# One product of the gate placed three sums later in every group, the mask counted earlier, one set of weight sums and two copies placed later

## The chip, the core and the metric

The kernel runs on one core of one Trainium2 chip. Five engines work side by side: TensorE (PE; its weight loads are listed as PEld), VectorE (DVE), ScalarE (ACT), GpSimd (POOL) and SyncE (SP, which only issues transfers here). The metric is the device time of one execution in microseconds, taken as the median of three runs.

## The reference

For 2 x 1024 tokens of 512 features, a layer norm is followed by two branches: a linear layer whose weight is multiplied by a 32 x 32 block mask, and a gated feed-forward layer with 1792 inner features. Their product is added to the input.

```python
xn = _layernorm(x, axis=-1)
# masked linear: a 32x32 block of the weight is kept where its mask sums to more than 0
block_mask = mask.reshape(nb, BLOCK_H, kb, BLOCK_W).astype(jnp.float32).sum(axis=(1, 3)) > 0
...
s = jnp.einsum('bsk,nk->bsn', xn, weight * elem_mask)
# feed-forward
var = jnp.mean(jnp.square(xn), axis=-1, keepdims=True)
nx = xn * jax.lax.rsqrt(var + RMS_EPS) * ln_w
g = jnp.einsum('bsh,ih->bsi', nx, gate_w)
u = jnp.einsum('bsh,ih->bsi', nx, up_w)
f = jnp.einsum('bsi,hi->bsh', jax.nn.silu(g) * u, down_w)
return x + s * silu(f)
```

## The kernel before

**The arithmetic.** All matrices are float32. A matrix product is cut into 2 x 2 blocks and done with seven block products instead of eight, and each of these is again cut into 2 x 2 and done with seven. The outer seven are called q (lists `OUTER` and `BLOCKS`), the inner seven m. One inner product is a 128 x 128 weight times a 128 x 512 operand (128 features by 512 tokens). The price of the saving is sums and differences: of the weights (`inner_a` on POOL, 128 columns at a time, and `outer_a`), of the activations (`outer_b`, `inner_b` on DVE and POOL), and of the products (`instance`, on DVE and ACT).

**The stages.** There are seven groups g of 256 inner features, gate and up together, and an eighth group, the masked linear layer. First the outer products q = 1 and 2 of all eight groups run, then q = 6, 5, 7, 3, 4 of group 0, of group 1 and so on. Each (g, q) is an *instance* j with seven products, so a group in the second stage takes 5 instances or 35 products. Then the down projection follows, seven sets of 25 products (`down_instance`, line 640).

**The order.** It is written out by hand. `at(pos, fn)` files a piece of work under a position; all pieces are sorted by position, and each engine runs its own pieces in exactly that order. One unit of position is one product on PE; instance j has positions 7j to 7j+6 and on, and its products stand at 7j + 0, 2, 3, 4, 6, 8, 12. Position 0 is about 14 us after the start. An instruction that waits holds back everything behind it on its engine, and SP's transfers are such a queue too. In this text "p148" means position 148.

**One instance** (`instance`). Product m = 1 goes to a PSUM bank x; ACT copies it to a bank z (`seed`, L399); m = 5 goes to a bank y, m = 2 is added to z. A copy of a bank is taken before the bank is added to again: m = 6 is added to x, and one position later `snap` (DVE, or ACT where there is nothing to add) writes bank plus an earlier partial result to SBUF; then m = 7 and m = 4 are added to the same bank. The same is done with y. `total` writes the four results. So a later product of the instance must wait until a `snap` or `total` has read its bank. PSUM has three banks of the kind X, two Y, one Z and two V. V serves everything else.

**The gate of a group** (`group`). When the four tiles of one output (R, Hh) are there, `silu` (ACT) puts silu of a gate tile into a V bank, and `h_out` (L463, DVE) multiplies it with the up tile and stores the product to DRAM by a transfer of SP. Output (1, 1) needs another sum first: for q = 7, `summed` adds acc to v5 for its tiles 0 and 1 on DVE and for 2 and 3 on POOL. The dictionary `hpos` holds the position of each `h_out`. `h_sum` (POOL) takes differences of these products, at positions worked out from `hpos`.

**Held copies.** `outer_b_held` lets ACT copy one operand into a V bank (`hold`, L249) and then DVE subtract with it (`outer_b`), 0.9 positions later.

**The mask.** `load_mask` loads four 128 x 512 tiles into the slots q.0 to q.3, free until the first group's blocks are loaded at p83. `mask_rows` (L349, DVE) sums 32 columns at a time; `mask_blocks` (p79.5) does the rest on PE and DVE.

**The start.** Tokens are loaded, normalised on ACT and DVE (L153/L155), transposed on PE (L162), and the first two instances (j = 0, 1) are run with positions of their own (`EARLY`). `inner_b(q, m)` makes the operands of q = 1 and 2: the list at line 777 has them with their positions and engines. `inner_a(0, 1, K, 1)` makes the four weight sums s1, s2, s4, s3 of q = K + 1 on POOL.

Of the kernel before, what the change touches and what calls it, by code (L numbers as in the profile page):

```python
# [31 lines left out]
def tile_masked_linear_gated_ffn(  # L32
# [36 lines left out]
    def at(pos, fn, *args):  # L69
        events.append((pos, len(events), fn, args))  # L70
# [18 lines left out]
    def slots(i, n):  # L89
        return mem[:, i : i + n, :]  # L90
# [3 lines left out]
    def bank(tag, name):  # L94
        return ps.tile([P, W], F32, tag=tag, name=name, bufs=PSB[tag])

    def add(eng, o, a, b, op=ALU.add):
        eng.tensor_tensor(o, a, b, op)  # L98

    dve, pool, act = nc.vector, nc.gpsimd, nc.scalar  # L100
# [150 lines left out]
    def outer_b_held(pos, lag, q, k, n):  # L251
        v = {7: lambda: u12[k, n], 6: lambda: raw[k, n], 5: lambda: raw[2 + k, 2 + n]}[q]
        at(pos - lag, hold, (q, k, n), v)
        at(pos, outer_b, q, k, n, dve)
# [39 lines left out]
    def w_slots(g):  # L294

        return (F["s"], F["s"] + 5) if g % 2 else (F["q"], F["a1"] + 4)
# [59 lines left out]
    def mask_a(v, R, K):  # L356
        v = v.rearrange("p (b j) -> p b j", j=BLK)
        k = keep[:, 2 * R + K, :].unsqueeze(2).to_broadcast([P, 16, BLK])
        nc.gpsimd.tensor_tensor(v, v, k, ALU.mult)

    def inner_a(g, part, k0=0, n=2):

        if part == 1:
            i, si, qs = F["a1"] + 2 * (g % 3), F["s"] + 2 * (g % 2), (1, 2)
        else:
            i, si, qs = *w_slots(g), BLOCKS
        a, s = slots(i + k0, n), slots(si + k0, n)
        a11, a21, a12, a22 = (a[:, :, k * P : (k + 1) * P] for k in range(4))
        s1, s2, s3, s4 = (s[:, :, k * P : (k + 1) * P] for k in range(4))
        for k in range(n):  # L370
            aop[g, qs[k0 + k]] = {1: a11[:, k], 2: a12[:, k], 3: s4[:, k], 4: a22[:, k],
                                  5: s1[:, k], 6: s2[:, k], 7: s3[:, k]}
        return [lambda: add(pool, s1, a21, a22), lambda: add(pool, s2, s1, a11, ALU.subtract),
                lambda: add(pool, s4, a12, s2, ALU.subtract), lambda: add(pool, s3, a11, a21, ALU.subtract)]
# [72 lines left out]
    def group(g, where):  # L447
        def tiles(i):
            return lambda k: mem[:, i + k, :]

        acc, v5, c1 = tiles(F["acc"] + 4 * (g % 2)), tiles(F["v5"] + 4 * (g % 2)), tiles(F["c1"] if g % 2 else F["vc"])
        vc = tiles(F["tmp"] + 2 if g % 2 else F["vc"])
        h11 = tiles(F["a1"])
        gate = {}

        def silu(key, t):
            gate[key] = bank("V", f"gate_{g}_{key[2]}")
            nc.scalar.activation(gate[key], t(), AF.Silu)  # L458

        hs, hpos = {}, {}  # L460

        def h_out(key, a, b, n):
            nc.vector.tensor_mul(a(), gate[key], b())  # L463
            hs[key] = a()
            q = {(0, 0): 1, (1, 0): 2, (1, 1): 3}.get(key[:2])
            if q:
                nc.sync.dma_start(h_dram[HD[q], g, n], a())

        def done(R, Hh, tiles):

            ready = {}

            def after(i, pos):
                r, n = divmod(i, 2)
                if g == G:
                    at(pos + 1, lambda: nc.sync.dma_start(s_dram[2 * R + r, 2 * Hh + n], tiles(i)))
                    return
                ready[i] = pos
                if n in ready and n + 2 in ready:
                    key = (R, Hh, n)  # L480
                    p = max(ready[n] + 1.2, ready[n + 2] - 0.5, SILU)
                    at(p, silu, key, lambda: tiles(n))
                    hpos[key] = max(p, ready[n + 2]) + 1.3
                    at(hpos[key], h_out, key, lambda: tiles(n), lambda: tiles(n + 2), n)
            return after

        def summed(dst, src, into, then=None, engines=(pool,) * 4):

            def after(i, pos):
                at(pos + 1.2, lambda: add(engines[i], into(i), dst(i), src(i)))  # L490
                if then:
                    then(i, pos + 3.2)
            return after

        nothing = lambda i, pos: None
        setup = {
            1: (None, acc, nothing),
            2: (acc, c1, done(0, 0, c1)),
            6: (acc, acc, nothing),
            5: (None, v5, summed(v5, acc, vc)),  # L500
            7: (acc, acc, summed(v5, acc, v5, done(1, 1, v5), (dve, dve, pool, pool) if g < G else (pool,) * 4)),
            3: (vc, vc, done(0, 1, vc)),
            4: (acc, acc, done(1, 0, acc)),
        }
        for q in setup:
            instance(where[g, q], g, q, *setup[q])

        def h_sum(q, n, tile_of, a, b):

            o = hs[q, n] = tile_of()  # L510
            add(pool, o, hs[a + (n,)], hs[b + (n,)], ALU.subtract)
            nc.sync.dma_start(h_dram[HD[q], g, n], o)

        sums, rest = slots(F["acc"] + 4 * (g % 2), 4), 7 * where[g, BLOCKS[0]]
        at(7 * where[g, 1] + 15, lambda: nc.sync.dma_start(acc_dram[g], sums))
        at(rest - (14 if g else 6), lambda: nc.sync.dma_start(sums, acc_dram[g]))
        if g < G:
            def again():
                nc.sync.dma_start(slots(F["a1"], 2), h_dram[HD[1], g].rearrange("n p w -> p n w"))
                hs.update({(0, 0, n): h11(n) for n in range(2)})  # L520
            at(rest + 24, again)
            pos = 0
            for n in (1, 0):
                for q, t, i, a, b in ((5, vc, n + 2, (0, 1), (0, 0)), (7, v5, n + 2, (1, 1), (0, 1)),
                                      (6, vc, n, (1, 1), (5,))):
                    pos = max(pos, hpos[0, 1, n], hpos[1, 1, n]) + 1.45
                    at(pos, h_sum, q, n, lambda t=t, i=i: t(i), a, b)
            for n in (1, 0):
                pos = max(pos, hpos[1, 0, n]) + 1.45
                at(pos, h_sum, 4, n, lambda n=n: acc(n + 2), (1, 0), (6,))  # L530
# [195 lines left out]
    T = lambda us: (us - 14.0) / 0.86  # L726
# [19 lines left out]
    def plan(pos, step, todo):  # L746
        for i, fn in enumerate(todo):
            at(pos + step * i, fn)
# [26 lines left out]
        at(T((9.75, 10.3, 10.85, 12.05)[c]), evacuate, 0, c, act)  # L775
        at((5.6, T(15.6), 6.0, 3.14)[c], evacuate, 1, c, act)
    for pos, q, m, eng in ((1.1, 1, 5, dve), (1.87, 1, 6, dve), (2.56, 1, 7, dve), (3.95, 2, 5, dve), (2.7, 1, 4, pool),
                           (4.6, 2, 6, dve), (7.2, 2, 7, dve), (5.0, 2, 4, pool)):
        at(pos, inner_b, q, m, eng)
    for q in (1, 2):  # L780
        for k in (0, 1):
# [20 lines left out]
        at(61 + k, outer_b, 4, k, 1, pool)  # L802
        at(67 + 1.3 * k, outer_b, 4, k, 0, pool)
    for pos, lag, q, k, n in ((51.0, 0.9, 5, 0, 1), (53.0, 0.9, 5, 1, 1), (57.2, 0.9, 7, 0, 0), (58.5, 0.9, 6, 0, 0), (60.3, 0.9, 7, 1, 0),
                              (61.4, 0.9, 6, 1, 0), (64.2, 0.9, 5, 0, 0), (65.6, 0.9, 5, 1, 0)):
        outer_b_held(pos, lag, q, k, n)
    for k in (0, 1):
        for n in (0, 1):
# [12 lines left out]
    for g in range(G + 1):  # L821
        p, rest = 7 * where[g, 1], 7 * where[g, BLOCKS[0]]
        for K in range(2):
            if g > 2:
                at(p - 22, load_a, g, K)
            if g == G:
                at(p - (10.4, 7.3)[K], lambda K=K: mask_a(aq[G, 0, K], 0, K))
            elif g > 1:
                at(p - (10.4, 7.3)[K], scale_a, g, K)
        if g:  # L830
            plan(p - 7, 1, inner_a(g, 1))
        else:
            plan(T(9.9), 0, inner_a(0, 1, 0, 1))
            plan(T(11.9), 0, inner_a(0, 1, 1, 1))
        at(rest - 29, load_block, g)

        def block_sums(g=g):
            for k, fn in enumerate(outer_a(g)):
                todo[g, k] = fn
        at(rest - 20, block_sums)  # L840
        if g == G:
            for k, (R, K) in ((1, (1, 0)), (4, (1, 1)), (0, (0, 0)), (3, (0, 1))):
                at(rest - 20.5, lambda k=k, R=R, K=K: mask_a(wblk[G][k], R, K))
        for k, off in enumerate((-19.9, -19.3, -18.1, -17, -15.95, -15.94, -15.93, -15.3, -13.95)):
            at(rest + off, lambda g=g, k=k: todo[g, k]())
        plan(rest - 13, 2.5, inner_a(g, 2, 0, 5))
# [1 line left out]
        for off, fn in zip((8, 24.6, 26.05, 26.06, 26.07, 27.5, 30), outer_d(f)):  # L848
            at(7 * where[f, BLOCKS[0]] + off, fn)
    for i, (R, K) in enumerate(QUADS):  # L850
        at(50, load_mask, R, K)
        at(62 + 3.5 * i, mask_rows, R, K)
    at(79.5, mask_blocks)
    at(120, rms_store)
    for t in range(NTT):
# [129 lines left out]
```

## Time and profile before

| | |
|---|---|
| median of three runs | 510.44 us (510.37 to 510.63) |
| the profiled execution | 510.38 us |
| its span, first to last instruction | 508.6 us, so 1.8 us lie outside it |
| TensorE clock granted | 0.999 |
| product x, two matmul records (L392) | 595 ns each; alone a pair is listed with 1.02 us, and pairs follow each other every 0.86 us |
| DVE sum with a PSUM input, 128 x 512 (L98) | 683 ns; back to back one starts every 0.60 us |
| DVE product h_out (L463) | 682 ns, 56 of them |
| mask_rows (L349) | 0.67 to 0.68 us, four of them |
| POOL sum 128 x 512 | 1.27 to 1.29 us |
| POOL sum 128 x 128 (first weight sums) | 0.45 to 0.51 us |
| ACT copy to or from a bank | 0.55 to 0.60 us |

PE's records overlap: a float32 product is two records that each begin before the one ahead has ended. So the starts of the products have to be read, not their busy time. In an answer of the timeline a line with x2 is one product, x4 two products; the columns are the start, the time from there to the last end, engine, line, operation, tiles, number of instructions and, in brackets, the idle time ahead of it and what ended it.

### The profile page before, as it was taken

What the parts mean: (1) busy time and instruction counts of PE and PEld (TensorE: products, weight loads), DVE (VectorE), ACT (ScalarE), POOL (GpSimd) and SP (SyncE); (2) the same over time, 40 slices, a digit from 0 to 9 for tenths busy, and PEclk for the clock granted to TensorE, in tenths of its full rate; (3) what the DMA queues carried; (4) which work ended last, traced back from release to release, by engine and by line L of the source; (5) the groups of instructions that cost most, each with busy time, mean ns of one, the idle gap of its engine ahead of it and who ended that gap; (6) DMA issues with size and microseconds to landing.
All of it is one profiled execution on the core that took longest, in us unless ns stands there. A gap on an engine that the chain in (4) does not pass through costs nothing. (4 is left out here: it accounts for less than half of the span.)

```text
span 508.6 us, 4930 instructions
## 1 busy us (share of the span) xinstructions
PE 502.6 (99%) x1237; PEld 227.2 (45%) x1237; DVE 376.4 (74%) x583; ACT 188.4 (37%) x361; POOL 358.6 (71%) x300
## 2 busy tenths in 40 slices
PE   8999999999999999999999999999999999999996
PEld 7444434444444444444444444444444444444444
DVE  6978798776978969697796969969747644377636
ACT  5656776634535363352635334330100101001111
POOL 4628997473786959879596889976672764649960
PEclk9999999999999999999999999999999999999999
DMA  6758866269178495866939566599996798467362
GB/s 206 249 189 337 315 227 253 89 256 321 48 242 310 179 309 198 284 250 225 348 145 312 198 236 231 202 337 378 356 343 244 230 394 307 134 247 254 120 226 84
DMA packets 62221, 124.75 MB, mean 245 GB/s; under 512 B 5968, under 2 KB 13552, under 8 KB 60144
## 3 DMA queue, kind: packets, MB, share of 16 engines
q1 hardware_dynamic: 62048, 124.43, 68.6%
q8 instruction: 10, 0.16, 0.1%
q14 instruction: 19, 0.16, 0.1%
q10 hardware_dynamic: 144, 0.00, 0.0%
HBM read 78.25 MB, written 46.15 MB: 245 GB/s over the span
## 5 line engine op out<-in xcount | busy, mean ns | idle before, releaser
L98 POOL TENSOR_TENSOR mem<-mem 128x512 f32<-128x512 f32 (+4 forms) x261 | 322.3, 1258 | 115.1 <-ACT mem L420 32.3
L392 PE MATMUL x<-mem 128*128 128x512 f32 x448 | 213.8, 595 | 0.7 <-DVE mem L98 0.4
L392 PEld LDWEIGHTS x<-mem 128*128 128x128 f32 x448 | 83.8, 190 | 110.3 <-issue 85.8
L98 DVE TENSOR_TENSOR mem<-x,mem 128x512 f32<-128x512 f32 x137 | 92.5, 683 | 42.6 <-PE x L392 39.1
L392 PE MATMUL y<-mem 128*128 128x512 f32 x224 | 114.7, 593 | 0.1
L640 PE MATMUL dx<-mem 128*128 128x512 f32 x174 | 78.3, 592 | 0.0
L98 DVE TENSOR_TENSOR mem<-mem 128x1536 f32<-128x1536 f32 (+3 forms) x50 | 66.3, 1332 | 6.9 <-PE dx L640 4.4
L98 DVE TENSOR_TENSOR mem<-y,mem 128x512 f32<-128x512 f32 x96 | 65.6, 684 | 6.8 <-PE y L392 5.3
L392 PEld LDWEIGHTS y<-mem 128*128 128x128 f32 x224 | 42.2, 190 | 53.7 <-issue 48.3
L399 ACT COPY z<-x 128x512 f32<-128x512 f32 x54 | 30.9, 572 | 91.9 <-PE x L392 88.9
L392 PE MATMUL z<-mem 128*128 128x512 f32 x112 | 57.4, 594 | 0.0
L640 PEld LDWEIGHTS dx<-mem 128*128 128x128 f32 x174 | 33.1, 190 | 41.6 <-issue 40.7
L640 PE MATMUL dy<-mem 128*128 128x512 f32 x98 | 44.5, 592 | 0.0
L463 DVE TENSOR_TENSOR mem<-gate,mem 128x512 f32<-128x512 f32 x56 | 38.1, 682 | 5.9 <-POOL mem L98 3.6
L458 ACT ACTIVATE gate<-mem 128x512 f32<-128x512 f32 x56 | 33.1, 601 | 24.8 <-DVE mem L98 20.3
L613 POOL TENSOR_TENSOR mem<-mem 128x512 f32<-128x512 f32 x16 | 25.6, 1609 | 14.0 <-DMA mem<-s_dram 13.8
L623 ACT ACTIVATE silu<-mem 128x512 f32<-128x512 f32 x15 | 9.0, 602 | 64.6 <-DVE mem L98 48.3
L392 PEld LDWEIGHTS z<-mem 128*128 128x128 f32 x112 | 21.0, 190 | 26.3 <-issue 23.3
L98 DVE TENSOR_TENSOR mem<-z,mem 128x512 f32<-128x512 f32 x41 | 28.0, 683 | 2.8 <-PE z L392 2.7
L640 PEld LDWEIGHTS dy<-mem 128*128 128x128 f32 x98 | 18.6, 190 | 23.4 <-issue 23.2
L98 DVE TENSOR_TENSOR mem<-dx,mem 128x512 f32<-128x512 f32 x16 | 11.1, 691 | 20.5 <-PE dx L640 20.4
L640 PE MATMUL dz<-mem 128*128 128x512 f32 x56 | 25.2, 592 | 0.0
(85 smaller groups left out, 290.3 us busy)
## 6 DMA issues: line engine op xcount, KB each, us to landing
h_dram<-mem SPq DMA_DIRECT2D x98, 256.0 KB, 2.1
mem<-h_dram SPq DMA_DIRECT2D x28, 768.0 KB, 6.3
mem<-in_gu SPq DMA_DIRECT2D x42, 256.0 KB, 3.9
acc_dram<-mem SPq DMA_DIRECT2D x8, 1024.0 KB, 4.3
mem<-acc_dram SPq DMA_DIRECT2D x8, 1024.0 KB, 5.8
mem<-in_x_t SPq DMA_DIRECT2D x24, 256.0 KB, 5.9
mem<-in_x SPq DMA_DIRECT2D x16, 256.0 KB, 4.4
s_dram<-mem SPq DMA_DIRECT2D x16, 256.0 KB, 5.1
```

The source lines that it names most:

```text
L98: eng.tensor_tensor(o, a, b, op)
L392: nc.tensor.matmul(st[key], weights(g, q, m), operand(q, m), start=first and not (key == "z" and seeded), stop=True, skip_group_check=True)
L399: nc.scalar.copy(st["z"], st["x"])
L458: nc.scalar.activation(gate[key], t(), AF.Silu)
L463: nc.vector.tensor_mul(a(), gate[key], b())
L613: at_later.append(lambda: nc.gpsimd.tensor_tensor(s_tile, s_tile, rms_bc[t], ALU.mult))
L623: nc.scalar.activation(b[0][:, part], y[:, part] if source is None else source(), AF.Silu)
L640: nc.tensor.matmul(st[key], w(), b(), start=first and key != "z", stop=True, skip_group_check=True)
```

## The change

Five edits of positions; no instruction is added, removed or given to another engine.

```diff
-                    hpos[key] = max(p, ready[n + 2]) + 1.3
+                    hpos[key] = max(p, ready[n + 2]) + (3.9 if key == (1, 1, 0) else 1.3)
                     at(hpos[key], h_out, key, lambda: tiles(n), lambda: tiles(n + 2), n)
...
-                           (4.6, 2, 6, dve), (7.2, 2, 7, dve), (5.0, 2, 4, pool)):
+                           (4.6, 2, 6, dve), (9.05, 2, 7, dve), (5.0, 2, 4, pool)):
         at(pos, inner_b, q, m, eng)
...
-                              (61.4, 0.9, 6, 1, 0), (64.2, 0.9, 5, 0, 0), (65.6, 0.9, 5, 1, 0)):
+                              (61.4, 0.9, 6, 1, 0), (65.1, 1.0, 5, 0, 0), (66.3, 1.3, 5, 1, 0)):
         outer_b_held(pos, lag, q, k, n)
...
-            plan(T(11.9), 0, inner_a(0, 1, 1, 1))
+            plan(2.75, 0, inner_a(0, 1, 1, 1))
...
     for i, (R, K) in enumerate(QUADS):
-        at(50, load_mask, R, K)
-        at(62 + 3.5 * i, mask_rows, R, K)
+        at(15 + 1.2 * i, load_mask, R, K)
+        at((46.1, 48.1, 50.2, 52.6)[i], mask_rows, R, K)
```

In every group the `h_out` of output (1, 1), token tile 0, is filed 2.6 positions later, with the transfer it issues; in group 0 that is p146.1 instead of p143.5. The difference `inner_b(2, 7)` goes from p7.2 to p9.05 on DVE. The two held copies of q = 5 move from p63.3 and p64.7 to p64.1 and p65.0 on ACT, the sums that use them from p64.2 and p65.6 to p65.1 and p66.3 on DVE. POOL's weight sums of q = 2, group 0, go from p-2.4 to p2.75. The four mask loads go from p50 to p15.0 to p18.6 on SP, the four counts from p62, 65.5, 69, 72.5 to p46.1, 48.1, 50.2, 52.6 on DVE.

## The prediction

> **What bounds the kernel now.** I read the busy times first, then PE's waits, then the starts on PE's timeline, and at each irregular start the timelines of DVE and ACT.
>
> ```profile
> PE 502.6 (99%) x1237; PEld 227.2 (45%) x1237; DVE 376.4 (74%) x583; ACT 188.4 (37%) x361; POOL 358.6 (71%) x300
> ```
>
> PE is busy 99% of the span, and the list of PE's waits has only 1.3 us at the start and this:
>
> ```profile
> PE x L392 <- DVE mem L98: 0.4, 1, 0.4
> ```
>
> That would leave 0.4 us to win. But the records overlap, so a late product need not leave idle time. In a smooth stretch a product starts every 0.86 us: one has a length of 1.02, two together 1.88. I looked for longer ones. The first kind returns in every group; PE around group 0's gate:
>
> ```profile
> 139.29 1.02 PE L392 MATMUL y<-mem 128*128 128x512 f32 x2
> 140.15 2.12 PE L392 MATMUL x<-mem 128*128 128x512 f32 x4
> 142.11 1.02 PE L392 MATMUL y<-mem 128*128 128x512 f32 x2
> ```
>
> 140.15 to 142.11 is 1.96 for two products that take 1.72: 0.24 lost. The second of the two is p148, which adds to the bank that the `snap` at p145 reads. DVE there:
>
> ```profile
> 137.91 0.68 DVE L463 TENSOR_TENSOR mem<-gate,mem 128x512 f32<-128x512 f32 x1
> 139.21 0.69 DVE L463 TENSOR_TENSOR mem<-gate,mem 128x512 f32<-128x512 f32 x1 [0.61 <-POOL mem L98]
> 139.81 0.68 DVE L98 TENSOR_TENSOR mem<-z,mem 128x512 f32<-128x512 f32 x1
> 140.41 1.28 DVE L98 TENSOR_TENSOR mem<-x,mem 128x512 f32<-128x512 f32 x2
> ```
>
> The `h_out` of (1, 1, 0) stands idle 0.61 us for POOL's sum of tile 2, and the `snap` (first of the pair at 140.41) ends at 141.10, with p148 starting at 141.15. The same 2.12 (2.11 once) stands at 170.43, 200.72, 231.00 and on; the last group is worse:
>
> ```profile
> 322.07 2.29 PE L392 MATMUL x<-mem 128*128 128x512 f32 x4
> 324.20 1.02 PE L392 MATMUL y<-mem 128*128 128x512 f32 x2
> ```
>
> 324.20 - 322.07 = 2.13 against 1.72: 0.41. The second kind is around p66 to p71:
>
> ```profile
> 68.89 1.02 PE L392 MATMUL y<-mem 128*128 128x512 f32 x2
> 69.87 1.12 PE L392 MATMUL z<-mem 128*128 128x512 f32 x2
> 70.83 1.88 PE L392 MATMUL x<-mem 128*128 128x512 f32 x4
> 72.68 1.12 PE L392 MATMUL y<-mem 128*128 128x512 f32 x2
> 73.64 1.96 PE L392 MATMUL x<-mem 128*128 128x512 f32 x4
> 75.44 1.02 PE L392 MATMUL y<-mem 128*128 128x512 f32 x2
> ```
>
> 68.89 to 75.44 is 6.55 for seven products (7 x 0.858 = 6.01): 0.54 lost. At 69.87 PE waits for ACT's `seed` (69.27 to 69.82), which stood behind a `hold` at 68.75; at 72.68 for this `snap`, the last line:
>
> ```profile
> 70.76 0.67 DVE L349 TENSOR_REDUCE mask_sums<-mem 128x16 f32<-128x512 int32 x1
> 71.35 0.68 DVE L98 TENSOR_TENSOR mem<-held,mem 128x512 f32<-128x512 f32 x1
> 71.95 0.68 DVE L98 TENSOR_TENSOR mem<-y,mem 128x512 f32<-128x512 f32 x1
> ```
>
> A mask count and a held sum stand ahead of it. The third is the start: PE's p12 starts at 23.10 after p11 at 21.64 (0.60 lost), waiting for DVE's `total` of p9, which had `inner_b(2, 7)` ahead of it:
>
> ```profile
> 21.67 0.68 DVE L98 TENSOR_TENSOR mem<-mem,pt 128x512 f32<-128x512 f32 x1
> 22.27 0.68 DVE L98 TENSOR_TENSOR mem<-x,mem 128x512 f32<-128x512 f32 x1
> 23.05 0.69 DVE L98 TENSOR_TENSOR mem<-y,mem 128x512 f32<-128x512 f32 x1
> ```
>
> From 324 to 501 PE has no irregular start, so time won before then should arrive at the end.
>
> **What the Trainium skill says.** Perfetto Trace Analysis, Identifying the Most-Contended Engine: PE's busy share is no good measure of headroom, because of pipelining. The trace agrees: 99% hides the losses above. PSUM — Partial Sum Buffer, Engine vs sequencer instructions: the queues of ScalarE, VectorE and GpSimd are strict FIFO; the 0.61 us wait above passing on to a `snap` whose own inputs were ready is just that. The same page, PSUM bank collisions: engines must be kept apart on one bank, reads too; here PE's p148 starts 0.05 after the bank's reader ends. SBUF — State Buffer, Who interferes with whom: DVE's tensor_scalar can contend with GpSimd, a DVE sum with one SBUF input does not. The trace agrees: DVE's halves of `normalise` took 0.44 to 0.61 beside POOL's sums at 14 to 16 us; sums with a PSUM input take 0.68 with POOL busy or idle.
>
> **The change part by part.** PE times are those of before, so each part is a shift.
>
> *The gate's product.* At p146.1 it follows `total` p144, `snap` p145, `total` p146. With DVE starting one sum each 0.60 us and PE's ends known, `total` p144 starts at 138.52, the `snap` at 139.12 (ends 139.80), `total` p146 at 139.72, the product at 140.35; POOL's tile was there at 139.18, so the wait is gone. p148 may start at 141.01, 1.2 after the `snap`. Next on DVE, `total` p147 starts at 140.95 instead of 141.61, so nothing behind is later. The gate's V bank is held until 141.03; its next user, the `silu` at p148.5, started at 142.32. The store moves 1.1 us and past one `h_sum` store on SP (issued 141.93), so to about 142.3; its DRAM tile is read only in the down stage, and `h_sum` positions do not move (p147.65 is already later than p146.1). In group 6 the same sequence gives the `snap` an end of 321.9 against p148's counterpart due at 322.93. Gain 6 x 0.24 + 0.41 = 1.85; bounds 0.87 of it (a small remainder in each group) and all.
>
> *Counts and held copies, where they leave.* The `seed` goes ahead of the `hold`: it starts about 68.75, ends 69.30, due 69.75. On DVE without the count: held sum 69.88 (after a `hold` at 69.27 to 69.86), `snap` p66 at 70.48, ends 71.16, due 72.32; the `snap` of p68 ends 73.56, due 74.0. Gain 0.54, bounds 0.3 and 0.54.
>
> *The counts, where they arrive.* DVE idles 1.08 us before 54.50: the first count fits at 53.32. From there, one start each 0.60: count 55.10, `total` 55.70, `h_out` 56.30, count 56.88, held sum 57.48, `total` 58.08, `snap` 58.86 (its input is the `total`, as now), count 59.46, held sum 60.05, `total` 60.65, `snap` p54 61.25 to 61.93. PE's p57 adds to that bank at 62.02 and needs 0.05 after the reader: some 0.04 of cover. If it is missed, a stall as in the groups, 0.1 to 0.25. I take 0. DVE has caught up by 63.08, where it idled 0.38. The loads: SP has nothing to do between the token loads (17.55) and 24.84, so one mask load leaves at about 18.0 and three after the 1 MB store at 24.84; with some 0.45 us per issue, the weight load at 25.27 leaves 1.4 later. It is used by ACT at about 41, landing was 29.9. Nothing.
>
> *The start.* `inner_b(2, 7)` behind `total` p9 puts that at 21.67, end 22.35, and p12 starts when PE reaches it, 22.50. The next late one is `snap` p10 (bank Y), now third: 22.87 to 23.55 against 23.05 to 23.74. p13 is due 23.36 and gets about 23.62, plus 0.10 in its second half as at every such restart. p14 then comes at 24.58 instead of 24.89: gain 0.31. POOL's sums now run after `inner_b(1, 4)` ends at 18.73, four of 0.5 one after the other, to 20.7; PE needs the first at 20.7 (there at 19.2) and the second at 21.6 (19.7). Without them at 14 to 16, DVE's `normalise` ends up to 0.4 earlier, but the next DVE sum that matters waits for ACT's copy at 16.05 to 16.64: 0.05 more. Together 0.35, bounds 0.15 and 0.6.
>
> Sum: 1.85 + 0.54 + 0.35 = 2.74. Against the profiled 510.38 that is 507.64, with a span of 505.9; the median was 0.06 higher, so **507.7 us**.
>
> **The rivals.** *The gains come only in part:* the counts meet p57, or the start moves its whole wait to `snap` p10. For it: the 0.04 of cover, and a DVE full from 16 to 24 us. Against: each is one stall. 507.7 + 0.25 + 0.3 + some 0.1 = 508.3. *The wait in the groups is replaced:* another reader (ACT's `seed`, or POOL's weights) ends as late as the `snap` did. For it: POOL runs without a gap from 134 to 143. Against: its weights for p149 and p150 were finished at 140.7, and ACT was idle 2 us before the `seed` at 141.21. Only 0.9 remains: 509.5. *Slower:* SP's queue. A mask load that has to wait for a transfer ahead of it (the last token load shows such a wait, ending at 17.53) holds the loads behind it: the weights and the transposed tokens. POOL uses the latter from 40.68 on, and they land from 33.7 on, with 5.8 us at POOL's next weight sums before PE needs those. It decides from a delay of 7 + 5.8 = 13 us on; 17 us would cost 4 on PE, less the 2.7 won, +1.3: 511.7. Nothing in the trace waits so long.
>
> **How the numbers follow.** Forecast 0.74, partial 0.12, replaced 0.08, slower 0.06. Low: everything at its upper bound, 510.44 - 3.0, with a little for the run: 507.2. High: the partial case and 0.5 over it, 508.8; 0.14 is left outside. A change of under 0.2% (1.0 us) would be none that a measurement can tell: 509.5 is 0.18% faster, so of the replaced case 0.06 counts as same and 0.02 as faster; slower 0.06, faster 0.88.
>
> **What would show it.** Right: the 2.12 gone at each group's p148 and groups 30.03 apart rather than 30.28; no brackets of 0.61 at L463; seven even products from 68 to 75; p12 after p11 by 0.86 and a small late start at p13. Wrong: a late p57, about 0.35 less than 62.02; a new long pair in each group; POOL or DVE waiting for transfers from 40 us on.

## The result, and the profile after

The changed kernel takes 507.86 us (median of five runs, 507.54 to 507.97) against 510.63 us for the kernel before, measured beside it (five runs, 510.37 to 511.12). The ratio is 0.9944, with a 95% interval of 0.9930 to 0.9959: faster by 0.4 to 0.7%. The forecast was 507.7 us with a range of 507.2 to 508.8. The profiled span fell from 508.6 to 505.8 us (forecast 505.9).

The busy times of the page, after:

```profile
PE 500.3 (99%) x1237; PEld 228.0 (45%) x1237; DVE 377.2 (75%) x583; ACT 187.6 (37%) x361; POOL 358.9 (71%) x300
```

PE's share is 99% again, though 2.8 us of the span have gone: the share tells nothing here. The starts do. (0.14 of the 2.8 us lie ahead of all moved work: DVE's reciprocal before `normalise`, L143, starts at 13.46 instead of 13.60.) PE's timeline after the change, around group 0's gate:

```profile
138.32 1.02 PE L392 MATMUL y<-mem 128*128 128x512 f32 x2
139.18 1.88 PE L392 MATMUL x<-mem 128*128 128x512 f32 x4
140.90 1.02 PE L392 MATMUL y<-mem 128*128 128x512 f32 x2
```

The pair that was 2.12 long is 1.88, and 139.18 to 140.90 is 1.72, two products without a loss. DVE's timeline there:

```profile
136.95 0.68 DVE L463 TENSOR_TENSOR mem<-gate,mem 128x512 f32<-128x512 f32 x1
137.55 0.68 DVE L98 TENSOR_TENSOR mem<-z,mem 128x512 f32<-128x512 f32 x1
138.15 1.28 DVE L98 TENSOR_TENSOR mem<-x,mem 128x512 f32<-128x512 f32 x2
139.35 0.68 DVE L463 TENSOR_TENSOR mem<-gate,mem 128x512 f32<-128x512 f32 x1
```

No idle time stands in brackets any more: sums start every 0.60 us, and the product (139.35) follows behind three of them. The `snap` that PE waits for is the first of the pair at 138.15. On the page the line of these 56 products shows the wait gone in sum too (it had 5.9 us of idle time, most of it ended by POOL):

```profile
L463 DVE TENSOR_TENSOR mem<-gate,mem 128x512 f32<-128x512 f32 x56 | 38.1, 682 | 1.9 <-ACT gate L458 1.4
```

PE where the counts and held copies were, p65 to p72:

```profile
68.47 1.02 PE L392 MATMUL y<-mem 128*128 128x512 f32 x2
69.32 1.02 PE L392 MATMUL z<-mem 128*128 128x512 f32 x2
70.18 1.88 PE L392 MATMUL x<-mem 128*128 128x512 f32 x4
71.90 1.02 PE L392 MATMUL y<-mem 128*128 128x512 f32 x2
72.76 1.88 PE L392 MATMUL x<-mem 128*128 128x512 f32 x4
74.47 1.02 PE L392 MATMUL y<-mem 128*128 128x512 f32 x2
```

68.47 to 74.47 is 6.00 for seven products: nothing is lost. Three late places remain. PE at the start, p9 to p14:

```profile
20.47 1.10 PE L392 MATMUL y<-mem 128*128 128x512 f32 x2
21.40 1.89 PE L392 MATMUL x<-mem 128*128 128x512 f32 x4
23.45 1.10 PE L392 MATMUL y<-mem 128*128 128x512 f32 x2 [0.16 <-DVE mem L98]
24.39 1.88 PE L392 MATMUL x<-mem 128*128 128x512 f32 x4
```

p11 and p12 now follow each other (x4, 1.89), and p13 at 23.45 is the late one: 0.32, and 0.08 in its second record, for the `snap` of p10. The second place is PE's p57, where the counts have gone:

```profile
60.66 1.96 PE L392 MATMUL x<-mem 128*128 128x512 f32 x4
62.46 1.02 PE L392 MATMUL y<-mem 128*128 128x512 f32 x2
```

1.80 for two products, 0.08 lost, all of it in p57's second record. The third is p348 at 311.81 (0.20 lost); it was late by 0.21 before, the prediction does not list it, and the change does not touch it.

### The profile page after: what moved, and what is told of

The parts are those of the page before. It is cut to its first block, busy times and chain, and to the rows that moved or that the text cites. A ratio compares the mean times of both kernels' runs of the same rounds, so it can differ in the third digit from the quotient of the medians.

```text
span 505.8 us, 4938 instructions
## 1 busy us (share of the span) xinstructions
PE 500.3 (99%) x1237; PEld 228.0 (45%) x1237; DVE 377.2 (75%) x583; ACT 187.6 (37%) x361; POOL 358.9 (71%) x300
## 4 chain that ended last, share of the span: by engine, by line
PE 94%; DVE 4%; ACT 1%; DMA 1%; issue 0%; DVEq 0%
PE x L392 37%; PE y L392 19%; PE dx L640 15%; PE z L392 9%; PE dy L640 8%; PE dz L640 5%; DVE mem L98 2%; PE dv L640 1%; DVE st L127 1%; DMA mem<-in_x 1%; ACT mem L155 0%; DVE agg L128 0%; DVE mem L630 0%; DVE mem L153 0%; DVE scl L146 0%
```

## The experiments

All ratios are to the kernel before on the same chip. The losses are read from the starts of PE's records, 0.429 us apart in a smooth stretch.

**The gate's product alone.** From the kernel before:

```diff
-hpos[key] = max(p, ready[n + 2]) + 1.3
+hpos[key] = max(p, ready[n + 2]) + (3.9 if key == (1, 1, 0) else 1.3)
```

> The kernel before with only the gate's product (1, 1, 0) at 2.6 positions later. Theory (DVE's wait for POOL passes to the snap behind it, and from there to PE): the seven long pairs of products go, each group takes 30.03 us, the span falls by 1.85 us, and nothing else on PE's timeline changes (the late p12 at 23 us and the two late products at 69 to 73 us stay). Rival (the wait is replaced by another one just behind it): PE stays late by 0.1 us or more in each group, and the span falls by less than 1 us.

508.49 us, ratio 0.9958 (0.9944 to 0.9971), span 506.8: 1.8 us shorter. All seven late products are gone, 1.88 us by the starts, and the late ones at 23 and 70 to 73 us stand as they did (0.09 us lost at 48.8 is new and in this profile alone). PE around group 0's gate:

```profile
140.22 1.88 PE L392 MATMUL x<-mem 128*128 128x512 f32 x4
141.94 1.02 PE L392 MATMUL y<-mem 128*128 128x512 f32 x2
```

No second wait took the place of the first. This is two thirds of the change.

**The held copies alone.** From the kernel before:

```diff
-(64.2, 0.9, 5, 0, 0), (65.6, 0.9, 5, 1, 0)
+(65.1, 1.0, 5, 0, 0), (66.3, 1.3, 5, 1, 0)
```

> The kernel before with only the two held copies and their sums moved; the counts stay at p62 to p72.5. Theory (two separate causes: the copy ahead of ACT's seed, and too many pieces on DVE ahead of the snaps): the late p66 goes (0.23 us), p69 is in time too since one held sum now stands behind its snap, but the snap of p68, still with counts and held sum ahead of it, then ends at about 74.4 against a due time of 74.0, so 0.4 to 0.5 us come back at p71: the span changes by less than 0.2 us. Rival (the held copies are the only cause): all of the 0.54 us goes.

510.37 us, ratio 0.9996 (0.9988 to 1.0005): no change. PE:

```profile
69.91 1.02 PE L392 MATMUL z<-mem 128*128 128x512 f32 x2
70.76 1.88 PE L392 MATMUL x<-mem 128*128 128x512 f32 x4
72.48 1.02 PE L392 MATMUL y<-mem 128*128 128x512 f32 x2
73.34 1.02 PE L392 MATMUL x<-mem 128*128 128x512 f32 x2
74.63 1.12 PE L392 MATMUL x<-mem 128*128 128x512 f32 x2 [0.27 <-DVE mem L98]
75.59 1.02 PE L392 MATMUL y<-mem 128*128 128x512 f32 x2
```

p66 (69.91) and p69 (72.48) are in time, and p71, at 74.63, is late by 0.44 and 0.10: the whole 0.54 us in one place. The reader of its bank is the last line here, on DVE:

```profile
72.11 0.68 DVE L98 TENSOR_TENSOR mem<-held,mem 128x512 f32<-128x512 f32 x1
72.70 0.68 DVE L98 TENSOR_TENSOR mem<-z,mem 128x512 f32<-128x512 f32 x1
73.30 0.68 DVE L98 TENSOR_TENSOR mem<-held,mem 128x512 f32<-128x512 f32 x1
73.90 0.68 DVE L98 TENSOR_TENSOR mem<-x,mem 128x512 f32<-128x512 f32 x1
```

It ends at 74.58, 0.05 before p71. In both orders DVE had some 0.6 us too much in this stretch, about one count; the held copies needed the counts to leave.

**The mask alone.** From the kernel before:

```diff
-at(50, load_mask, R, K)
-at(62 + 3.5 * i, mask_rows, R, K)
+at(15 + 1.2 * i, load_mask, R, K)
+at((46.1, 48.1, 50.2, 52.6)[i], mask_rows, R, K)
```

> The kernel before with only the mask's loads and counts moved. Theory: the late p66 stays (0.23 us, it waits for ACT), the late p69 and the long second half at p71 go (0.31 us), and at p57 PE gets its bank just in time or up to 0.1 us late. Span 0.2 to 0.3 us shorter. Theory of the loads (the early loads hold up SP's queue): POOL and DVE wait for transfers between 40 and 55 us and PE gets late there; span longer.

510.13 us, ratio 0.9994 (0.9985 to 1.0002), which by itself settles nothing; the starts do. p69 and p71 are in time, p66 is late by 0.28 (ACT's `seed`, as before), p57 by 0.08: net about 0.2 us from p57 on. Between 24 and 62 us PE has no late start, so the early loads cost nothing.

**The start alone.** From the kernel before:

```diff
-(4.6, 2, 6, dve), (7.2, 2, 7, dve), (5.0, 2, 4, pool)
+(4.6, 2, 6, dve), (9.05, 2, 7, dve), (5.0, 2, 4, pool)
...
-plan(T(11.9), 0, inner_a(0, 1, 1, 1))
+plan(2.75, 0, inner_a(0, 1, 1, 1))
```

> The kernel before with only inner_b(2, 7) and POOL's second set of weight sums moved. Theory: p12 starts 0.86 us after p11, p13 is late by 0.3 us for the snap of its bank, DVE's halves of normalise take 0.40 us each where POOL's sums are gone; counted from the first transposes of the tokens' second tile (14.8 us before) p14 comes 0.3 to 0.4 us earlier, and the long pairs in the groups and around 69 us stay as they were. What PE does before 14 us isn't touched and may differ by some tenths from run to run with the landing of the first weight.

510.13 us, ratio 0.9993 (0.9986 to 1.0000), span 508.1. p12 follows p11, p13 is late by 0.33, and p14 comes at 24.36 against 24.89. Counted from the first transpose, as the expectation has it, p14 is 0.48 earlier, not 0.3 to 0.4; but 0.34 of the 0.53 us lie ahead of DVE's reciprocal (13.25 against 13.60), and PE reached the transposes late in this profile, 1.06 us after `normalise` began against 0.77. From p11 to p14, where neither counts, it is 2.99 instead of 3.25. The rest is as before. The time resolves this part no better than the mask's; each is under 0.1%.

**The product behind one sum.** From the changed kernel:

```diff
-(3.9 if key == (1, 1, 0) else 1.3)
+(2.3 if key == (1, 1, 0) else 1.3)
```

> The changed kernel with the gate's product (1, 1, 0) only 1.0 position later than before, behind one sum (total p144) instead of three. Theory (what counts is the order of this wait and the snap's end against PE's due time): the product starts when POOL's tile is there, DVE idles some 0.1 us, the snap behind it ends about 0.5 us before PE needs the bank, so no group has a late product and the time is the changed kernel's within 0.1 us. Rival (the product must stand behind the snap): part of the 0.24 us per group comes back, up to 1.85 us in all.

507.52 us, ratio 0.9943 (0.9929 to 0.9956), span 505.8: the same as three sums. DVE's timeline:

```profile
137.64 0.68 DVE L98 TENSOR_TENSOR mem<-z,mem 128x512 f32<-128x512 f32 x1
138.33 0.69 DVE L463 TENSOR_TENSOR mem<-gate,mem 128x512 f32<-128x512 f32 x1
138.94 1.28 DVE L98 TENSOR_TENSOR mem<-x,mem 128x512 f32<-128x512 f32 x2
```

One sum fills the time until POOL's tile is there; the wait shrinks from 0.61 to about 0.09 us, and the `snap` still ends ahead of PE's need. It isn't the number three that counts, nor that the product stands behind the `snap`.

**Two counts side by side.** From the changed kernel, the third count moved next to the fourth:

```diff
-(46.1, 48.1, 50.2, 52.6)
+(46.1, 48.1, 52.55, 52.6)
```

> The changed kernel with the third count moved from p50.2 to p52.55, next to the fourth, so that one more count of 0.6 us stands between the snap of p52 and the snap of p54. Theory (at p57 the cover is used up): PE's p57 is late by about 0.55 us and its second half by 0.10, where the changed kernel loses 0.08; span 0.57 us longer. Rival (the 0.08 us at p57 is not DVE's): no change at p57.

508.24 us, ratio 0.9958 (0.9944 to 0.9971), span 506.2. PE at p56, p57 and p58:

```profile
60.53 1.02 PE L392 MATMUL x<-mem 128*128 128x512 f32 x2
61.93 1.13 PE L392 MATMUL x<-mem 128*128 128x512 f32 x2 [0.38 <-DVE mem L98]
62.89 1.02 PE L392 MATMUL y<-mem 128*128 128x512 f32 x2
```

p57 is late by 0.55 and 0.10, that is 0.57 more than in the changed kernel. So one more count of 0.60 us appears nearly whole: the cover at p57 is used up, and the 0.08 is DVE's.

**POOL's weight sums back.** From the changed kernel:

```diff
-plan(2.75, 0, inner_a(0, 1, 1, 1))
+plan(T(11.9), 0, inner_a(0, 1, 1, 1))
```

> The changed kernel with POOL's second set of weight sums back at p-2.4. Theory: DVE's halves of normalise take 0.5 to 0.6 us again where they meet POOL's sums, DVE's second difference, inner_b(1, 6), waits for ACT's copy of its bank either way and starts 0.05 to 0.2 us later; p14 comes 0.05 to 0.2 us later than 24.39. Rival (the sums' place gives most of the gain at the start): p14 comes 0.3 us later or more.

507.63 us, ratio 0.9946 (0.9932 to 0.9959): the time does not tell it from the changed kernel. p14 comes at 24.81 instead of 24.39, which would be the rival's size. But part of that is not the sums': PE reached the transposes late here, 1.07 us after `normalise` began, against 0.66 in the changed kernel. The profile of the start alone has the same late PE (1.06) and no sums at this place, so it is the one to compare with. From DVE's reciprocal to p14 it takes 11.10 us, this kernel 11.27 and the changed kernel 10.93. So the sums' place is worth 0.17 us at p14 by this one pair, inside the first expectation, and PE's late start another 0.17. It is no fixed amount: from the reciprocal to p11 it is 8.11 with the mask alone, where the sums stand at their old place and PE was late too (1.06), and 8.12 with the start alone. The four halves of `normalise`, changed kernel first, then with the sums back:

```profile
13.87 1.38 DVE L153 TENSOR_SCALAR mem<-mem,scl,nb 128x256 f32<-128x256 f32 x4
```

```profile
14.08 1.95 DVE L153 TENSOR_SCALAR mem<-mem,scl,nb 128x256 f32<-128x256 f32 x4
```

Beside POOL's sums they take 1.95 us in all, without them 1.38. The instruction just ahead of them (L144) took 0.29 us here and 0.16 in the changed kernel.

**The next three late products.** From the changed kernel:

```diff
-(4.6, 2, 6, dve), (9.05, 2, 7, dve)
+(4.6, 2, 6, dve), (12.05, 2, 7, dve)
...
-at((46.1, 48.1, 50.2, 52.6)[i], mask_rows, R, K)
+at((46.1, 46.2, 48.1, 50.2)[i], mask_rows, R, K)
...
-at(pos + 1.2, lambda: add(engines[i], into(i), dst(i), src(i)))
+at(pos + (2.1 if (g, i) == (G - 1, 1) and engines[i] is dve else 1.2), lambda: add(engines[i], into(i), dst(i), src(i)))
```

> The changed kernel with its three remaining late products treated: inner_b(2, 7) at p12.05, behind the snaps of p10 and p12; the fourth count next to the first, at p46.2, where DVE idles, and the others moved up (p48.1, p50.2); in the last group only, the sum of tile 1 of q = 7 on DVE 0.9 positions later, behind the total of p345. Theory: the late p13 (0.40 us), p57 (0.08) and p348 (0.20) all go, the span falls by 0.65 to 0.7 us to 505.1, the time to 507.2. Rival (each of these waits has another one just behind it): less than 0.3 us is won.

508.15 us, ratio 0.9956 (0.9942 to 0.9969), span 506.5: nothing is won over the changed kernel (ratio 0.9944, 0.9930 to 0.9959). The theory fails: by the starts 0.68 are won and 0.97 lost. The rival's number holds, its reason at one of the three places: p13 and p57 are in time with no wait behind them, and p348 is in time too, but p349, right behind it, is late by 0.97 us. DVE and then POOL there:

```profile
310.42 0.68 DVE L98 TENSOR_TENSOR mem<-x,mem 128x512 f32<-128x512 f32 x1
311.01 1.71 DVE L98 TENSOR_TENSOR mem<-mem 128x512 f32<-128x512 f32 x1
312.64 0.68 DVE L98 TENSOR_TENSOR mem<-y,mem 128x512 f32<-128x512 f32 x1
```

```profile
310.64 1.54 POOL L98 TENSOR_TENSOR mem<-mem 128x640 f32<-128x640 f32 x1 [0.21 <-DVE mem L98]
```

The moved sum (311.01) has both inputs in SBUF, as its `mem<-mem` shows. POOL's weight sum had started at 310.64 and ends at 312.18; DVE's ends at 312.72, 0.54 after that, and the `snap` that PE's p349 needs stands behind it. In the changed kernel the same two met the other way round, DVE first at 310.48 (0.67 us), POOL at 310.70, and POOL was the slower one:

```profile
310.70 1.86 POOL L98 TENSOR_TENSOR mem<-mem 128x640 f32<-128x640 f32 x1 [0.21 <-DVE mem L98]
```

**Two of the three.** The kernel of the experiment before, without its last edit, and the changed kernel beside it on one chip:

> The run before without its third part: inner_b(2, 7) at p12.05 and the counts at p46.1, 46.2, 48.1, 50.2, the last group's sum back at its place. Theory (the 0.97 us lost at p349 there came from DVE's sum of two SBUF tiles standing beside POOL's weight sum, 1.71 us instead of 0.68): p349 is in time, p348 is late by 0.2 us as in the changed kernel, p13 and p57 stay in time; from p14 on the span is 0.1 us shorter than the changed kernel's and p14 itself comes 0.4 us earlier after p12; span 505.3 give or take 0.2 for the start. Rival (the earlier counts or the later difference caused the loss at p349): p349 is late again.

> The changed kernel itself, beside the run above on the same chip. Theory: the same late products as in its first profile (p13 0.40, p57 0.08, p348 0.20), and 0.4 to 0.5 us more time than the run above. Rival (what two parts win is lost elsewhere): the two times agree within 0.1 us.

507.07 us (506.98 to 507.20, five runs; ratio to the kernel before 0.9936, 0.9924 to 0.9949) against 507.76 us for the changed kernel (507.68 to 507.99; ratio 0.9951, 0.9937 to 0.9964). The two ranges do not meet: this version beats both kernels, the changed one by 0.7 us or 0.14%. p349 is in time and p348 is late by 0.20 again, so the loss at p349 was the moved sum's. The gain is more than the 0.4 to 0.5 us expected. PE's p11 to p15 in this version:

```profile
21.41 1.89 PE L392 MATMUL x<-mem 128*128 128x512 f32 x4
23.14 1.02 PE L392 MATMUL y<-mem 128*128 128x512 f32 x2
24.00 1.88 PE L392 MATMUL x<-mem 128*128 128x512 f32 x4
```

p13 comes at 23.14, 1.73 after p11, and p14 0.86 later: 0.40 less than in the changed kernel. By the starts 0.40 and 0.08 are won; the spans, 505.3 and 506.0, and the times differ by 0.7. In the two profiles the other 0.2 us lie ahead of p12. The medians differ by 0.7 too, and whether the 0.2 is this version's or chance stays open, since the other runs have no profile.

## Why the prediction was right

*The reading of PE.* Right: its list of waits offered 0.4 us, and 2.7 were there. The starts showed them, and the groups now follow each other after 30.04 us instead of 30.28.

*The gate's product.* Expected 1.85 us; alone it gave 1.88 by the starts and 1.8 of span. That the `snap` gets free, and that the later product and its store delay nobody, was read from the timelines ahead; both traces bear it out.

*Counts and held copies, where they leave.* Expected 0.54, measured 0.54 (6.55 against 6.00 us for the seven products). The experiments add that the two edits are not two gains: held alone wins 0.00, the mask alone 0.26 and both together 0.54, the last two less the 0.08 at p57.

*The counts, where they arrive.* The prediction gave 0.04 us of cover at p57 and took no loss; a late start of 0.1 to 0.25 was kept for the range. The loss was 0.08. The `snap` ended at 61.44 and p57 began at 61.52, 0.86 after p56 and so in time; it was its second record that came 0.08 late. The cover was sized right, 0.03 beyond the 0.05; the need was not. PE's weight load waits for the `snap` too and wants more time ahead of the product, as the last section shows.

*The start.* Expected 0.35 at p14; the two profiles differ by 0.50. Of these, 0.14 lie ahead of DVE's reciprocal, which starts between 13.25 and 13.88 in the twelve profiles; they are taken as chance. From there to p11, where of the moved work only POOL's sums can act, 0.10 are won (8.04 to 7.94 us), and 0.26 from p11 to p14, which is the difference (24.89 - 21.64 = 3.25 before, 24.39 - 21.40 = 2.99 after; the same 3.25 in the four profiles without it, the same 2.99 in the five with both edits of the start as they are). The forecast had 0.05 and 0.31: the mechanism was right, both terms are 0.05 off in opposite directions, and that the sum still agrees is luck. The term of the sums is the shakier one, between nothing and 0.17 in the pairs of the experiments.

*The sum.* By the starts the parts come to 1.88 + 0.54 - 0.08 + 0.36 = 2.70 against 2.74 expected; the span fell by 2.8, with the 0.14 of chance. That the span came out within 0.1 us of the forecast is partly luck too: the chance gain made up for the loss at p57.

*The rivals.* "Only in part" occurred as the 0.08 at p57, which the range allowed and the point did not, and the late p13, which was in the forecast. "Replaced" fell with the gate's product alone. The queue of SP showed nothing: PE had no late start from 24 to 62 us.

## What to carry to other kernels

Where an engine is busy 99% of the time, measure the distance of its starts against a smooth stretch; a wait of 0.14 us hides inside overlapping records, and the seven products of the gate lost 1.88 us that way, 0.37% of the time. A bank that is read just in time is read too late: by the estimate of the last section it had to be free 0.16 us ahead of the product here. An instruction that waits should stand behind everything that is ready and that the bottleneck needs next; one sum was enough here, which filled the time until the input was there. And when a stretch holds more work than fits, a new order only moves the late place, as the held copies showed; what helps is work taken out to where the engine idles.

## What the runs showed of the hardware

A late start costs twice: in all the late products of these runs the record after the late one came 0.08 to 0.10 us late too (0.14 and 0.10 in the groups, 0.55 and 0.10 with two counts), so a wait of 0.14 costs 0.24. The traces show where this comes from. PE's weight loads for p148 before, for p148 after and for p57 after:

```profile
141.14 0.30 PEld L392 LDWEIGHTS x<-mem 128*128 128x128 f32 x2 [0.81 <-DVE mem L98]
139.61 0.19 PEld L392 LDWEIGHTS x<-mem 128*128 128x128 f32 x1 [0.24 <-DVE mem L98]
61.49 0.30 PEld L392 LDWEIGHTS x<-mem 128*128 128x128 f32 x2 [0.64 <-DVE mem L98]
```

In a smooth stretch the load starts 0.43 us ahead of its product (139.61, the product at 140.04). Where the bank's reader ends later than that, the load waits for it too. In the groups before the change it starts 0.05 us after the reader (141.10), together with the late product (141.14 and 141.15). At p57 it starts 0.05 us after the reader (61.44) and 0.02 ahead of a product that is in time (61.49 and 61.52). In the twelve profiles, from 19 to 498 us, 99 products have a load that starts between 0.00 and 0.10 us ahead of them; in each, this lead and the lateness of the second record add up to 0.106 or 0.107 us. So, as an estimate from these traces, a bank that is free 0.16 us ahead of the product (0.05 and 0.11) costs nothing. Why the second record follows the load was not tested.

A DVE sum with two SBUF inputs took 0.68 us alone and 1.71 when POOL's sum of SBUF tiles was already running; with DVE first, POOL's took 1.86 instead of 1.54. The Trainium skill, SBUF — State Buffer, Who interferes with whom, says that such a pair contends. These two traces agree, and show that the one that comes second pays. I had used this page for DVE's `normalise` in the prediction, and had not looked for it when I placed that sum, although the trace of before has such a pair (310.73, 1.06 us). The same sum in the changed kernel, tile 0 of the last group:

```profile
308.30 1.05 DVE L98 TENSOR_TENSOR mem<-mem 128x512 f32<-128x512 f32 x1
```

POOL's sum had started at 307.54, and DVE's ended 0.54 us after it, as in the other trace. The sums behind follow every 0.60 us without a gap up to the `total` that p348 waits for (it ends at 311.76, p348 starts at 311.81). So the 0.20 lost at p348 seem to come from this pair; that was not tested.
